# A two-layer transformer on one core: layer 1's float gate and up products from split operands, and its input norms by pairs of row tiles

## The chip, the core and the metric

The kernel runs on one core of a Trainium2 chip. TensorE (PE in the profile) multiplies matrices out of SBUF into PSUM, VectorE (DVE) and ScalarE (ACT) work element by element on both, GpSimd (POOL) does so on SBUF, and SyncE (SP) issues transfers; GpSimd's own queue issues a few as well. Each engine runs its instructions in order, and semaphores tie the engines together. The metric is the device time of one execution in microseconds, as a median of several.

## What is computed

Four sequences of 256 tokens with 256 features pass through two layers, each with a mixer and a feed-forward part, and a LayerNorm after each of the four residual sums:

```
x = layernorm(x + L0_attn(x))      16 heads, rope, softmax
x = layernorm(x + L0_ffn(x))       W2 · fwht(silu(x W1ᵀ) * (x W3ᵀ)), 1024 wide
x = layernorm(x + L1_attn(x))      an mLSTM block with an MLP of its own, below
x = layernorm(x + L1_ffn(x))       int8 weights, 1024 wide

def L1_attn(x):
    h_in  = rmsnorm(x, norm1_w)
    q, k, v, o_pre = h_in @ wq, h_in @ wk, h_in @ wv, h_in @ w_og
    i_pre, f_pre   = soft_cap(h_in @ w_ig + b_ig), soft_cap(h_in @ w_fg + b_fg)
    h     = mlstm_parallel(q, k, v, i_pre, f_pre)          # 8 heads
    h_out = sigmoid(o_pre) * (rmsnorm of each head of h * mh_w)
    x1    = x + h_out @ w_out
    h2    = rmsnorm(x1, norm2_w)
    return x1 + (silu(h2 @ w_gate) * (h2 @ w_up)) @ w_down # 256 -> 1024 -> 256
```

The change is in the last line's two products, w_gate and w_up, and in the norms that lead to h_in and h2.

## The kernel before

Tokens go in two halves, n = 0 and n = 1, of 512 tokens, that is four row tiles of 128 (NJH = 4). Residual rows are token-major (`acc[n]`, `xb[n]`, `xs[n]`), the input of a product is feature-major (`fm`, two chunks of 128 features by 512 tokens). `transposed` (L794) makes the one from the other: four transposes for each chunk on TensorE, and one eviction that multiplies by the norm's weight on VectorE (L806).

*The feed-forward parts.* `glu` (L820) goes over the eight blocks c of 128 hidden features: one float32 product of two matmuls 128x512 for the gate and one for the up part (both recorded at the helper's L70), a tanh on ScalarE (L829), two operations on VectorE (L831, L832) that leave the gated block in `hT`. `fast_glu` (L847) does the same work by a Strassen scheme: for each pair of blocks, seven products at 128x256 (L871) on sums of weights (`hidden_sums`, L165) and of tokens (`token_sums`, L835 to L841) in place of eight. Layer 0 uses `fast_glu` for its half 0 and `glu` for half 1 (`ffn0`, L941). Layer 1's MLP uses `glu` for half 0 and `fast_glu` for half 1 (`ffn1`, L963). `down` (L925) is the product back to 256 features, eight float32 matmuls 128x256 for each row tile (L930). The int8 feed-forward part at the end (`ffn2_*`, from L1286) already uses float32r products on inputs in two parts (L1279).

*Norms.* `layernorm` (L770) and `rmsnorm` (L782) work on four row tiles at a time: bn_stats or a square with a sum on ScalarE (L787) for each tile, one chain of small VectorE steps for the reciprocal roots of all four (`rsqrt`, L51: 13 steps, of which 9 are three Newton rounds), then one scaling for each tile (L777, L790). The mLSTM's input is LayerNorm, root, RMSNorm, root; h2 is an RMSNorm of the rows that the product with w_out leaves (L1269).

*The order of the work.* The streams are generators that yield an amount of TensorE time. `merge` (L1382) emits pieces of one stream between those of another: the rest of `ffn0(1)` lies under `mlstm(0)`, the downs of `ffn0(1)` around `ffn1(0)`'s norm, the blocks of `ffn1(0)` under `mlstm(1)`, its downs around the head norm of half 1 and around h2_1's norm, and `ffn1(1)` then runs by itself, followed by the int8 part. A scheduler fixes the order on each engine when the kernel is built; emission order is its priority, and `behind` and `issue_after` are explicit orders. Inside `mlstm` stand: `mlstm_in` (L1009; transposes of hin, then w_if, w_qk, w_vo), gates and decays (GpSimd's L1153 is part of these, released by the "far" transfers on SP's queue), `attend` (L1178, L1195), `head_norm` (L1208 to L1228), transposes of `hos` and the product with w_out. `mix`, `late` and `work` are SBUF pools.

*Storage.* Large weights and sums share one pool tag "ff" with seven tiles of 1 MB that go round: wsum0, xsum, wsum1, w2b, w2, w1, w3, then gsum, gsum3 with tsum, w_up, w_gate, w_down and the three int8 weights q_gate, q_up (issued on GpSimd's queue when `ffn0(1)`'s downs are emitted) and q_down. PSUM has four banks under the tags "mm" and "sc" (tag "d" of the streams) and four under "pt" and "ot" (tag "m").

Of the kernel before, what the change touches and what calls it, by code (L numbers as in the profile page):

```python
# [17 lines left out]
P = 128  # L18
# [17 lines left out]
SWAP = [i ^ 1 for i in range(32)]  # L36


@with_exitstack
def tile_two_layers(ctx: ExitStack, tc: tile.TileContext, a: dict, out: bass.AP):  # L40
# [10 lines left out]
    def rsqrt(v, n, scale, eps):  # L51

        ve = small.tile([P, n], F32, tag="rs_v", name="rs_v")
        nc.vector.tensor_scalar(ve, v, scale, eps, ALU.mult, ALU.add)
        sh = small.tile([P, n], I32, tag="rs_sh", name="rs_sh")
# [83 lines left out]
    def ff_weight(name, engine=nc.sync, dtype=F32):  # L139

        tiled = [P, NH, D] if name in ("w2", "w_down", "q_down") else [P, KC, FF]
        t = wts.tile(tiled, dtype, tag="ff", name=name, bufs=7)
# [4 lines left out]
    pair_sums = lambda k: wts.tile([P, 4, 4 * P], F32, tag="ff", name=f"wsum{k}", bufs=7)  # L147
    wsums = [pair_sums(0)]
    xsum = wts.tile([P, 2, 4, S], F32, tag="ff", name="xsum", bufs=7)
    wsums.append(pair_sums(1))  # L150
    w2b = wts.tile([P, NH, D], F32, tag="ff", name="w2b", bufs=7)
    w2, w1, w3 = (ff_weight(k) for k in ("w2", "w1", "w3"))


# [492 lines left out]
    for h in range(NB - 1):  # L647
# [3 lines left out]
        if h == NB - 3:  # L651
            gsum = wts.tile([P, 2, 2, NH // 2, P], F32, tag="ff", name="gsum", bufs=7)
            with behind(settled["block"]):
                hidden_sums(nc.vector, (w1, w3), "first")
# [11 lines left out]
    both = wts.tile([P, 8 * S], F32, tag="ff", name="gsum3", bufs=7)  # L666
# [50 lines left out]
    mix = tc.alloc_tile_pool(name="mix", bufs=1, side="right")  # L717
# [44 lines left out]
    def hidden(n, pool):  # L762
        return pool.tile([P, NH, HALF], F32, tag="hT", name=f"hT{n}")
# [18 lines left out]
    def rmsnorm(src, dst):  # L782

        ss = small.tile([P, NJH], F32, tag="rms_ss", name="rms_ss")
        for j in range(NJH):
            junk = work.tile([P, D], F32, tag="junk", name="junk")
            nc.scalar.activation(junk, src[:, j, :], AF.Square, accum_out=ss[:, j : j + 1])  # L787
        rstd = rsqrt(ss, NJH, 1.0 / D, RMS_EPS)
        for j in range(NJH):
            nc.vector.tensor_scalar(  # L790
                dst[:, j, :], src[:, j, :], rstd[:, j : j + 1], None, ALU.mult
# [28 lines left out]
    def glu(xT, wg, wu, hT, tag):  # L820

        for c in range(NH):
# [9 lines left out]
            nc.vector.tensor_tensor(hT[:, c, :], pu, g, ALU.mult)  # L832
# [14 lines left out]
    def fast_glu(xT, wg, wu, hT, tag, spare, fourth, other):  # L847
# [4 lines left out]
        def pair(k):  # L852
# [23 lines left out]
            def places(c, b):  # L876
                if not g:
                    g.append(spare(k))
                return g[0][:, c, batch(b)], hT[:, 2 * k + c, batch(b)]
# [45 lines left out]
    def down(hT, wd, j, tag, rows, scale=0.5):  # L925

        po = bank(tag)[:, :D]
        for i in range(NH):
            fill(
                lambda: nc.tensor.matmul(  # L930
                    po, lhsT=hT[:, i, j * P : (j + 1) * P], rhs=wd[:, i, :],
# [9 lines left out]
    def ffn0(n, tag):  # L941
        fm = feature_major(n)
        if not n:
            rest = hidden(2, hid)
            four = rest[:, 0:2, :].rearrange("p x (k d) -> p x k d", d=P)
            hidden_sums(nc.gpsimd, (w1, w3), "fourth", four)
        hT = hidden(n, hid)
# [5 lines left out]
        if n:  # L953
            yield from glu(fm, w1, w3, hT, tag)
        else:
            token_sums(fm)
            room = lambda k: rest[:, 2 + 2 * (k % 2) : 4 + 2 * (k % 2), :]
            yield from fast_glu(fm, w1, w3, hT, tag, room, lambda x, k: four[:, x, k], rows[0])
        for j in range(NJH):
            yield from rows[j]  # L960
        layernorm(acc[n], xb[n])

    def ffn1(n, tag):  # L963

        h2 = work.tile([P, NJH, D], F32, tag="hin", name=f"h2_{n}")
        rmsnorm(acc[n], h2)
        yield 0.0
        fm, hT = feature_major(n), hidden(n, hid)
        evicted = transposed(h2, fm, tag, vecs[:, 4:6])
        if n:  # L970
            with tc.issue_after(evicted.ins):
                evicted = token_sums(fm)
            with tc.issue_after(evicted.ins):
                evicted = hidden_sums(nc.vector, (w_gate, w_up), "fourth")
        with tc.issue_after(evicted.ins):
            for j in range(NJH):
                nc.vector.tensor_tensor(xs[n][:, j, :], acc[n][:, j, :], xb[n][:, j, :], ALU.add)
        yield 0.9
        rows = [down(hT, w_down, j, tag, xs[n][:, j, :], 1.0 if n else 0.5) for j in range(NJH)]
        if n:  # L980
            room = lambda k: split.tile([P, 4, HALF], F32, tag="qx", name="gates")[:, 0:2]
            yield from fast_glu(
                fm, w_gate, w_up, hT, tag, room,
                lambda x, k: (w_gate, w_up)[x][:, 0, (2 * k + 1) * P : (2 * k + 2) * P], rows[0],
            )
        else:
            yield from glu(fm, w_gate, w_up, hT, tag)
        for j in range(NJH):
            yield from rows[j]
# [8 lines left out]
    ones = mix.tile([2 * 32, S], F32, tag="ones", name="ones")  # L998
    nc.gpsimd.memset(ones, 1.0)
    bias = mix.tile([P, 1], F32, tag="bias", name="bias")  # L1000
    nc.scalar.mul(bias, b_if, 1.0 / CAP)
    DV = DV1 + 1
    HV = H1 * DV
    own = mix.tile([P, H1], F32, tag="own", name="own")
    nc.vector.tensor_reduce(own, ident.rearrange("p (h d) -> p h d", h=H1), AX.X, ALU.add)
# [537 lines left out]
```

## Time and profile before

| | us |
|---|---|
| three runs | 694.25, 696.74, 696.4 |
| median of them | 696.4 |
| span of the profiled execution | 692.4 |
| time around that span (696.4 less 692.4) | 4.0 |
| layer 1 begins: transposes of hin, half 0 | 460.99 |
| `ffn1(0)`: first gate product | 523.85 |
| transposes of hin, half 1 | 536.44 |
| w_qk of half 1 | 540.32 |
| last product of `attend`, half 1 | 578.1 |
| transposes of h2_1 | 597.45 |
| `ffn1(1)`: first gate product | 599.40 |
| `ffn1(1)`: last gate or up product | 626.09 |
| int8 part: first product | 638.16 |
| end of the span | 692.4 |

Times are from the start of the span. In a line of the timeline the fields are: start, length, engine, line of the kernel, operation, output and inputs, shapes, number of instructions, and in brackets the idle time before them with what ended it. A float32 matmul leaves two records, a float32r matmul one; a record's length includes its way through the array, so the time of one is read from the distance of starts. In a line of windows the fields are: window and its length, then busy time with the number of instructions of PE, PEld, DVE, ACT and POOL, then the granted TensorE clock, the DMA share and GB/s.

### The profile page before, as it was taken

The numbers are of one execution on the slowest core, as the hardware profiler recorded it, in microseconds if no ns is written. First come the engines' busy times: TensorE is split into PE (matmuls) and PEld (weight loads), VectorE is DVE, ScalarE is ACT, GpSimd is POOL, SyncE is SP. The second block draws the span as 40 slices with busy tenths as digits, with TensorE's granted clock in tenths as the row PEclk, the third lists the DMA queues.
The fourth block names the chain that finished last, engine by engine and source line by source line (L and its number), as shares of the span: only waits on it lengthen the run. The fifth ranks groups of instructions, "written<-read, shape, count | busy, mean of one in ns | idle before, by whom it ended". The sixth has DMA issues, their size and how long they took to land.

```text
span 692.4 us, 10218 instructions
## 1 busy us (share of the span) xinstructions
PE 680.3 (98%) x3504; PEld 551.4 (80%) x3504; DVE 474.0 (68%) x1310; ACT 280.2 (40%) x839; POOL 183.0 (26%) x191
## 2 busy tenths in 40 slices
PE   9999999999999999999999999999999999999995
PEld 5888988988888898898888878845685568788785
DVE  5966766666477478467747786474779648966767
ACT  2442543344254254334425355136412561261652
POOL 3254314413431440441442920004100140000210
PEclk9999999999999999999999999999999999999998
DMA  8543233232331421520331322003031300001001
GB/s 270 216 123 61 39 100 62 54 95 51 67 96 36 108 66 26 138 57 17 64 62 28 96 47 87 1 0 124 1 121 62 120 4 1 0 1 62 0 1 62
DMA packets 49030, 45.46 MB, mean 66 GB/s; under 512 B 9521, under 2 KB 42705, under 8 KB 47825
## 3 DMA queue, kind: packets, MB, share of 16 engines
q1 hardware_dynamic: 48112, 41.00, 22.8%
q0 software_dynamic: 432, 3.15, 1.3%
q10 hardware_dynamic: 432, 0.66, 0.3%
q8 instruction: 28, 0.46, 0.3%
q14 instruction: 26, 0.20, 0.1%
HBM read 25.61 MB, written 1.08 MB: 39 GB/s over the span
## 4 chain that ended last, share of the span: by engine, by line
PE 88%; DVE 8%; ACT 2%; POOL 1%; issue 1%; DVEq 0%; ACTq 0%
PE ps_mm L371 13%; PE ps_mm L70 10%; PE ps_ot L70 8%; PE ps_d L70 7%; PE ps_sc L363 6%; PE ps_sc L371 6%; PE ps_d L930 4%; PE ps_d L1279 4%; PE ps_m L70 4%; PE ps_sc L455 4%; PE ps_pt L455 4%; PE ps_m L871 4%; PE ps_d L871 3%; PE ps_sc L467 2%; PE ps_m L930 2%; PE ps_m L1195 2%
## 5 line engine op out<-in xcount | busy, mean ns | idle before, releaser
L315 POOL TENSOR_TENSOR rope_raw<-rope_raw,cst 128x512 f32<-128x512 f32 x30 | 38.2, 1272 | 181.8 <-DVE rope_swp L312 181.8
L487 ACT ACTIVATE pr<-ps_sc,nmax 128x256 f32<-128x256 f32 x64 | 29.7, 475 | 121.3 <-DVE nmax L478 121.3
L70 PE MATMUL ps_mm<-w_o,oT 128*128 128x256 f32 x256 | 62.2, 379 | 0.0
L70 PE MATMUL ps_ot<-prT,v 128*128 128x256 f32 x240 | 61.4, 380 | 0.1
L569 DVE TENSOR_TENSOR acc<-ps_mm,acc 128x512 f32<-128x512 f32 x32 | 22.1, 690 | 48.3 <-PE ps_mm L70 48.3
L70 PEld LDWEIGHTS ps_mm<-w_o,oT 128*128 128x128 f32 x256 | 46.6, 190 | 5.3
L70 PEld LDWEIGHTS ps_ot<-prT,v 128*128 128x128 f32 x240 | 43.3, 190 | 5.5 <-issue 0.8
L1153 POOL TENSOR_TENSOR ex<-cst,ex 128x512 f32<-128x512 f32 x16 | 19.7, 1266 | 93.7 <-DMA ex<-far 93.7
L385 ACT COPY kn<-ps_sc 128x256 f32<-128x256 f32 x56 | 20.9, 373 | 58.3 <-PE ps_sc L363 58.2
L497 DVE TENSOR_SCALAR pr<-pr,rinv 128x256 f32<-128x256 f32 x128 | 42.8, 375 | 1.6
L371 PE MATMUL ps_mm<-xsum,wsum 128*128 128x256 f32 x180 | 43.9, 380 | 0.0
L505 DVE STREAM_TRANSPOSE cross<-pr 128x512 f32<-128x512 f32 x60 | 42.6, 711 | 1.4
L478 DVE TENSOR_REDUCE nmax<-ps_sc 128x2 f32<-128x512 f32 x32 | 20.6, 686 | 32.7 <-PE ps_sc L467 32.6
L316 POOL TENSOR_TENSOR rope_swp<-rope_swp,cst 128x512 f32<-128x512 f32 x30 | 38.1, 1270 | 0.0
L371 PEld LDWEIGHTS ps_mm<-xsum,wsum 128*128 128x128 f32 x180 | 33.9, 190 | 4.5
L394 DVE TENSOR_TENSOR kn<-ps_sc,kn 128x256 f32<-128x256 f32 x42 | 17.8, 423 | 28.5 <-ACT kn L385 18.1
L487 ACT ACTIVATE pr<-ps_pt,nmax 128x256 f32<-128x256 f32 x64 | 30.1, 489 | 2.6 <-DVE nmax L478 2.6
L455 PE MATMUL ps_sc<-kn,qn 128*128 128x256 f32 x128 | 30.2, 379 | 0.0
L455 PE MATMUL ps_pt<-kn,qn 128*128 128x256 f32 x128 | 30.2, 379 | 0.0
L70 PE MATMUL ps_d<-fm,w 128*128 128x512 f32 x64 | 29.4, 599 | 0.0
L930 PE MATMUL ps_d<-w,hT 128*128 128x256 f32 x128 | 28.4, 379 | 0.0
L363 PEld LDWEIGHTS ps_sc<-wsum,xsum 128*128 128x128 f32 x168 | 25.4, 191 | 2.2
(317 smaller groups left out, 1631.0 us busy)
## 6 DMA issues: line engine op xcount, KB each, us to landing
prT<-cross SPq DMA_DIRECT2D x240, 64.0 KB, 2.1
w_qkv<-in_w_qkv SPq DMA_DIRECT2D x7, 1024.0 KB, 7.0
ex<-far SPq DMA_DIRECT2D x8, 512.0 KB, 5.1
w<-in_w SPq DMA_DIRECT2D x3, 1024.0 KB, 11.6
w_o<-in_w_o SPq DMA_DIRECT2D x8, 256.0 KB, 3.3
acc<-in_x SPq DMA_DIRECT2D x2, 512.0 KB, 9.0
w_up<-in_w_up SPq DMA_DIRECT2D x1, 1024.0 KB, 4.9
w_gate<-in_w_gate SPq DMA_DIRECT2D x1, 1024.0 KB
```

The lines of the kernel that those rows point to most:

```text
L70: last = nc.tensor.matmul(ps, lhsT=lhs(i), rhs=rhs(i), start=(i == 0), stop=(i == n - 1))
L315: nc.gpsimd.tensor_tensor(by_b(raw[c]), by_b(raw[c]), cs, ALU.mult)
L316: nc.gpsimd.tensor_tensor(by_b(swp), by_b(swp), sn, ALU.mult)
L363: lambda: nc.tensor.matmul(ps[:, k * S + j * P : k * S + (j + 1) * P], lhsT=x[:, j * P : (j + 1) * P], rhs=wt, start=(start and not k and ...
L371: lambda: nc.tensor.matmul(ps[:, k * S : (k + 1) * S], lhsT=wt, rhs=x, start=(start and not k), stop=True, skip_group_check=True,)
L455: lambda: nc.tensor.matmul(ps[bb][e][:, qt * S : (qt + 1) * S], lhsT=qn[:, e, queries(bb, qt)], rhs=kn[:, e, keys(bb)], start=(qt == 0), s ...
L487: nc.scalar.activation(pr[:, qt, :], ps[:, qt * S : (qt + 1) * S], AF.Exp, bias=nmax[:, qt : qt + 1], accum_out=rsum[:, qt : qt + 1],)
L497: nc.vector.tensor_scalar(pr[:, qt, :], pr[:, qt, :], rinv[:, qt : qt + 1], None, ALU.mult)
L505: return nc.vector.transpose(cross[:, :, e], pr.rearrange("p t (x i) -> p x t i", i=32))
L871: nc.tensor.matmul(banks[name][:, batch(x)], lhsT=left, rhs=right, start=start and not x, stop=True, skip_group_check=True,)
L930: lambda: nc.tensor.matmul(po, lhsT=hT[:, i, j * P : (j + 1) * P], rhs=wd[:, i, :], start=(i == 0), stop=(i == NH - 1),)
L1279: nc.tensor.matmul(ps, lhsT=lhs, rhs=rhs, start=(k == 0), stop=(k == len(terms) - 1))
```

## The change

*Split operands.* `parts_of` clears the twelve low bits of a float32 operand for its top (a bitwise AND with −4096 on VectorE) and takes the rest exactly. With T, L the top and rest of a weight and t, l those of an input, three float32r operands are kept of each: T, L and T/4096 − L; t, 4096·l and t − 4096·l. `three_products` adds T·t + L·(4096 l) in one bank (P0, four matmuls 128x512 over the two feature chunks) and the product of the third parts in another (P1, two matmuls). Then (1 + 1/4096)·P0 − P1 = T·t + T·l + L·t + L·l. ScalarE takes the first term (`mul`), VectorE subtracts the second.

*Use.* `split_glu` takes this for the gate and up products of both halves of layer 1's MLP: per block c twelve matmuls into four banks. In half 0 the gate goes on by tanh, with the last product of gate and up on GpSimd; in half 1 by a silu on ScalarE, with that product on VectorE. `fast_glu` and its sums are no longer used in layer 1.

*Weights.* w_gate and w_up come in raw by quarters into the buffers of hin (SP's queue). The gate's quarters are split when `ffn0(1)`'s first two steps have been emitted, the up part's inside the first downs of `ffn0(1)`; the subtraction of a weight's top is on GpSimd. The pool "ff" has seven fixed places: gate parts in 3, 0, 1, up parts in 2, 5, 6 (those of wsum1, w1, w3), w_down in 4, the int8 weights in 0, 1, 2. These are therefore issued when the products of `ffn1(1)` are done, all three on GpSimd's queue. `hT` is eight tiles from a pool of ten instead of one; the int8 part's `hT` lies in quarters in freed places.

*Norms.* `mlstm_rows` does the LayerNorm and the RMSNorm of the mLSTM's input for a pair of row tiles with one chain for both roots, right behind those tiles' downs. `mlp_rows` does h2's RMSNorm for a pair right behind its products with w_out. `mlstm_in`'s yield ahead of the transposes goes from 9.0 and 10.5 to 5.0, that ahead of `ffn1(1)`'s transposes from 6.0 to 4.3.

```diff
+TOP = -4096
+STEP = 2.0**-12
...
+    def slot(k, shape, name, dtype=F32):
+        return wts.tile(shape, dtype, tag=f"ff{k}", name=name)
...
-    w_up, w_gate = ff_weight("w_up"), ff_weight("w_gate")
+    def raw_weights(name):
+        staged = [work.tile([P, 2, KC, S], F32, tag="hin", name=f"raw_{name}") for _ in range(2)]
+        quarters = [t[:, k] for t in staged for k in range(2)]
+        for q, t in enumerate(quarters):
+            nc.sync.dma_start(t, a[name][:, :, q * S : (q + 1) * S])
+        return quarters
+    raw_gate = raw_weights("w_gate")
...
+    def parts_of(src, to, scaled, engine):
+        low, fine = to[1], to[2]
+        top = work.tile([P, HALF], F32, tag="glu_t", name="top")
+        top = top.rearrange("p (a b) -> p a b", b=src.shape[-1]) if len(src.shape) == 3 else top
+        nc.vector.tensor_single_scalar(top.bitcast(I32), src.bitcast(I32), TOP, ALU.bitwise_and)
+        if scaled:
+            nc.vector.tensor_tensor(src, src, top, ALU.subtract)
+            nc.scalar.mul(low, src, 1.0 / STEP)
+            nc.vector.tensor_tensor(fine, top, low.bitcast(F32), ALU.subtract)
+        else:
+            engine.tensor_tensor(low, src, top, ALU.subtract)
+            nc.vector.scalar_tensor_tensor(fine, top, STEP, low.bitcast(F32), ALU.mult, ALU.subtract)
+        nc.scalar.copy(to[0], top)
+    def weight_parts(raw, to, q):
+        parts_of(raw[q], [t[:, :, q * S : (q + 1) * S] for t in to], False, nc.gpsimd)
+    def input_parts(fm):
+        x = work.tile([P, 3, KC, HALF], F32R, tag="parts", name="parts", bufs=1)
+        for c in range(KC):
+            parts_of(fm[:, c, :], [x[:, k, c, :] for k in range(3)], True, nc.vector)
+        return x
+    def three_products(ps, w, x, c):
+        cols = slice(c * P, (c + 1) * P)
+        for at, ks in ((0, (0, 1)), (1, (2,))):
+            terms = [(w[k][:, i, cols], x[:, k, i, :]) for i in range(KC) for k in ks]
+            for m, (left, right) in enumerate(terms):
+                last = nc.tensor.matmul(ps[at], lhsT=left, rhs=right, start=(m == 0), stop=(m == len(terms) - 1))
+        return last
+    def whole(dst, ps):
+        nc.scalar.mul(dst, ps[0], 1.0 + STEP)
+        nc.vector.tensor_tensor(dst, dst, ps[1], ALU.subtract)
+    def split_glu(x, wg, wu, hT, tag, smooth):
+        for c in range(NH):
+            pg, pu = [bank(tag) for _ in range(2)], [bank(tag) for _ in range(2)]
+            fill(lambda: three_products(pg, wg, x, c))
+            yield 1.35
+            fill(lambda: three_products(pu, wu, x, c))
+            z = work.tile([P, HALF], F32, tag="glu_g", name="glu_g")
+            nc.scalar.mul(z, pg[0], 1.0 + STEP)
+            with behind(weighed[-1]) if weighed and not smooth else contextlib.nullcontext():
+                nc.vector.tensor_tensor(z, z, pg[1], ALU.subtract)
+            if smooth:
+                nc.scalar.activation(z, z, AF.Silu)
+                whole(hT[c], pu)
+                nc.vector.tensor_tensor(hT[c], hT[c], z, ALU.mult)
+            else:
+                g = work.tile([P, HALF], F32, tag="glu_t", name="glu_t")
+                evictions.append(nc.scalar.activation(g, z, AF.Tanh, scale=0.5))
+                whole(hT[c], pu)
+                nc.vector.scalar_tensor_tensor(z, g, 1.0, z, ALU.add, ALU.mult)
+                nc.gpsimd.tensor_tensor(hT[c], hT[c], z, ALU.mult)
+            yield 1.35
...
+    def mlstm_rows(n, j):
+        if n not in entry:
+            entry[n] = work.tile([P, NJH, D], F32, tag="hin", name=f"hin{n}")
+        mv = small.tile([P, 2, 2], F32, tag="ln_mv", name="in_mv")
+        for k in range(2):
+            statistics(acc[n][:, j + k, :], mv[:, k, :])
+        ve = small.tile([P, 4], F32, tag="rs_v", name="rs_v")
+        nc.vector.tensor_scalar(ve[:, 0:2], mv[:, :, 1], 1.0 + RMS_EPS, RMS_EPS * LN_EPS, ALU.mult, ALU.add)
+        nc.vector.tensor_scalar(ve[:, 2:4], mv[:, :, 1], LN_EPS, None, ALU.add)
+        y = root(ve, 4)
...
+    def mlp_rows(n, j):
...
+            nc.scalar.activation(junk, acc[n][:, j + k, :], AF.Square, accum_out=ss[:, k : k + 1])
+        rstd = rsqrt(ss, 2, 1.0 / D, RMS_EPS)
...
     def ffn0(n, tag):
...
-            yield from glu(fm, w1, w3, hT, tag)
+            for k, wait in enumerate(glu(fm, w1, w3, hT, tag)):
+                if k == NH:
+                    raw_up = raw_weights("w_up")
+                yield wait
+            kept["up"] = [slot(k, [P, KC, FF], f"up{k}", F32R) for k in (2, 5, 6)]
...
         for j in range(NJH):
-            yield from rows[j]
-        layernorm(acc[n], xb[n])
+            for wait in rows[j]:
+                if n and j < 2:
+                    weight_parts(raw_up, kept["up"], splits.pop(0))
+                yield wait
+            if j % 2:
+                mlstm_rows(n, j - 1)
...
     def ffn1(n, tag):
-        rmsnorm(acc[n], h2)
-        yield 0.0
-        evicted = transposed(h2, fm, tag, vecs[:, 4:6])
...
+        transposed(mlp[n], fm, tag, vecs[:, 4:6])
+        x = input_parts(fm)
...
+        yield from split_glu(x, kept["gate"], kept["up"], hT, tag, bool(n))
...
+            if j % 2:
+                mlp_rows(n, j - 1)
...
-    merge(chain(take(1, one), [4.3]), other)
+    merge([4.3], other)
...
-    w_down = ff_weight("w_down")
-    q_gate, q_up = (ff_weight(k, nc.gpsimd, F32R) for k in ("q_gate", "q_up"))
+    w_down = ff_weight("w_down", 4)
...
-    merge(chain(take(1, one), [6.0]), left)
+    merge([4.3], left)
+    run(take(1, one))
     run(left)
-    run(take(1 + len(STEPS), one))
-    q_down = ff_weight("q_down", nc.gpsimd, F32R)
+    run(take(2 * NH, one))
+    q_gate, q_up, q_down = (ff_weight(name, k, nc.gpsimd, F32R) for k, name in enumerate(("q_gate", "q_up", "q_down")))
```

More of the change, by code (lines that the diff above doesn't have):

```diff
@@ L651, in tile_two_layers @@
         if h == NB - 3:
[L652 removed]
+            gsum = slot(0, [P, 2, 2, NH // 2, P], "gsum")
             with behind(settled["block"]):
@@ L959, in ffn0 @@
+            yield from fast_glu(fm, w1, w3, hT, tag, gates, lambda x, k: four[:, x, k], rows[0])
         for j in range(NJH):
-            yield from rows[j]
-        layernorm(acc[n], xb[n])
-    def ffn1(n, tag):
-        h2 = work.tile([P, NJH, D], F32, tag="hin", name=f"h2_{n}")
-        rmsnorm(acc[n], h2)
-        yield 0.0
-        fm, hT = feature_major(n), hidden(n, hid)
-        evicted = transposed(h2, fm, tag, vecs[:, 4:6])
[L970 to L977, printed above, removed]
-        yield 0.9
[L979 to L987, printed above, removed]
@@ L988, in ffn1 @@
         for j in range(NJH):
-            yield from rows[j]
+            yield from down(hT, w_down, j, tag, xs[n][:, j, :], 1.0 if n else 0.5)
             if j % 2:
                 layernorm(xs[n][:, j - 1 : j + 1], xb[n][:, j - 1 : j + 1], 2)
[L998 to L1004, printed above, removed]
@@ L1096, in gates @@
         nc.vector.tensor_scalar_mul(neg, last, -1.0)
-        summed = nc.vector.tensor_tensor(lsp, fcum, gmax, ALU.add)
-        if n:
-            with behind(summed):
-                hidden_sums(nc.vector, (w_gate, w_up), "first")
+        nc.vector.tensor_tensor(lsp, fcum, gmax, ALU.add)
         nc.scalar.activation(fac[:, 0:P], g[:, 0:P], AF.Exp, bias=neg)
```

112 lines of the change are left out of this document (68 added, 44 removed).

## The prediction

> **What bounds the kernel now.** I read the busy table first, then the chain that ended last, then that chain in order of time over layer 1, then TensorE's timeline at the stages that the diff touches, and the clock in the tail.
>
> ```profile
> PE 680.3 (98%) x3504; PEld 551.4 (80%) x3504; DVE 474.0 (68%) x1310; ACT 280.2 (40%) x839; POOL 183.0 (26%) x191
> ...
> PE 88%; DVE 8%; ACT 2%; POOL 1%; issue 1%; DVEq 0%; ACTq 0%
> ```
>
> TensorE is the bound over the whole span, so a product saved is time saved wherever its stage has no other chain of the same length. The second look is at those places:
>
> ```profile
> 597.45 1.13 PE ps_m L799 x7
> 598.60 0.76 DVE fm L806
> 599.40 8.32 PE ps_m L871 x36
> 607.83 14.81 PE ps_m L871 x68
> 622.64 1.73 PE ps_m L930 x8
> 624.37 1.73 PE ps_m L871 x8
> ...
> 645.80 16.37 PE ps_d L1279 x72
> ```
>
> The columns are start, length, engine, tile, line, records. The reader is to see that the second half's gate and up products (L871) are one run of TensorE, entered through one eviction of VectorE (L806), and that the int8 FFN's products, already float32r, come at 16.37/72 = 0.2274 us.
>
> ```profile
> 523.85 1.99 PE L70 MATMUL ps_d<-fm,w_gate 128*128 128x512 f32 x4 [0.41 <-DVE fm L806]
> 525.67 1.88 PE L70 MATMUL ps_d<-fm,w_up 128*128 128x512 f32 x4
> 527.39 1.88 PE L70 MATMUL ps_d<-fm,w_gate 128*128 128x512 f32 x4
> ...
> 597.45 1.23 PE L799 MATMUL ps_m<-cst,h 128*128 128x128 f32 x8 [0.90 <-DVE h L790]
> 598.51 0.60 PE L1292 MATMUL ps_d<-cst,xb 128*128 128x128 f32 x4
> 599.40 0.70 PE L871 MATMUL ps_m<-fm,w_gate 128*128 128x256 f32 x2 [0.30 <-DVE fm L806]
> ```
>
> In the first half a float32 block (gate or up, one of 16) takes 527.39 − 525.67 = 1.72 us. Idle time of TensorE is small and lies exactly where the change puts more work on VectorE: 0.41 and 0.30 us before the two GLUs, 0.90 before h2_1's transposes.
>
> **The change, part by part** (line numbers are those of the kernel before; prices not shown above are means of its groups by shape).
>
> 1. *Products, first half.* Sixteen blocks of 1.72 = 27.5 us become sixteen of six float32r matmuls, 96 x 0.2274 = 21.8: **−5.7**.
>
> 2. *Products, second half.* Before, 8.32 + 14.81 + 1.73 and 0.11 between them = 24.97 us (seven products instead of eight, at 128x256). After, again 21.8: **−3.1**. Had the seven-product form gone on in the first half too, there would be less to save; as it is the two sum to −8.8.
>
> 3. *Weight parts.* A quarter of a weight is a bitwise AND on VectorE, a subtraction on GpSimd, one fused op on VectorE, one copy on ScalarE. Prices: L790 (128x256, SBUF to SBUF, scalar operand) comes every 0.285 us, so 0.57 for 512; the fused op as L831, 0.68; the subtraction as L1153 on GpSimd, 1.27; the copy as the cast L1295, 0.59. The four gate quarters (VectorE 5.0, GpSimd 5.1 us) are issued beside layer 0's second GLU, where VectorE is busy 8.6 of the 10.3 us from 449.7 and 27.1 of the 45 after it: the second stretch covers them, 0; without it 5.0. The up quarters take the tiles of w1 and w3, whose last product is at about 504, so in the built order their steps stand in VectorE's queue between the root and the gating of mLSTM half 0's head norm, and hos's second pair of transposes waits behind one quarter's AND and fused op: 0.57 + 0.68 = 1.25, **+1.2** (bounds 0, if the downs in TensorE's queue cover it, and 5.0 for four quarters).
>
> 4. *Input parts, first half.* Behind each eviction come AND 0.57, a subtraction 0.68, a scaling on ScalarE 0.59, a subtraction 0.68 and a copy 0.59. The first product needs eviction, AND and copy: 1.16 more than now; the corrections follow 1.9 us behind it. Eight downs (8 x 0.43 = 3.45 us) stand before it in the built order. I take 0.4 for the start and 0.6 for the wait on the corrections: **+1.0** (0.4 to 2.4).
>
> 5. *Norms by pairs.* The mLSTM's LayerNorm and RMSNorm share one root, and nothing is left between the last down and the transposes but one pair. The 0.30 us before hin1's transposes goes, since 4.5 pairs of blocks now fit ahead of them: **−0.4** with the neighbouring 0.1 (0 to −0.9).
>
> 6. *Cover in mLSTM half 1.* Before, eight blocks, 13.8 us, fill its waits; after, by my walk, 41 matmuls, 9.3 us. That is where the first half's saving is cashed, if the stage's own chain allows it. VectorE is busy 22.7 of its 37.8 us and ScalarE 21.1, so neither is the limit by throughput; but single 0.23-us matmuls now stand where a 1.72 block covered a VectorE step, and hT's product of gate and up is on GpSimd behind eight L1153 of 1.27. I take **+0.6** (0 to +4.5, all of the lost cover).
>
> 7. *Entry of the second half's GLU.* In the built order VectorE runs two rows of xb0, one residual add and one bn_stats between the two pairs' roots; h2_1 ends some 0.8 later than now, 599.0. Then evictions 2 x 0.70, AND 0.57, copy 0.59: first product at about 602.2 instead of 599.4, last correction of the second chunk at 604.8, and four products of 0.2274 behind it: the first pair of blocks ends at 605.7. Seven pairs of 2.73 end at 624.8; undelayed from 599.4 they would end at 621.2. That is 3.6; two of the steps overlap by records' tails of 0.1 to 0.2, so **+3.3** (1.2, the bare eviction-AND-copy, to 4.5).
>
> 8. *Evictions.* A pair of blocks takes TensorE 2.73, ScalarE three ops of 0.6 (1.8), VectorE three of 0.69 (2.07), GpSimd 1.27: TensorE remains longest, 0. Were VectorE held up by over 0.66 us in each pair it would be the bound.
>
> 9. *Removed:* sums for seven products (L172 and its kin, eight of 0.68 on VectorE), token sums (L838 to L841), copies: all beside TensorE's run, 0. *Moved transfers:* w_up and w_gate raw in quarters on SP's queue ahead of the far transfers; the three q weights on GpSimd's queue behind the GLU instead of far ahead. A q weight lands 4.8 us after its issue (4.6 for q_down), and the second half's downs give 32 x 0.43 = 13.8 us cover; q_gate and q_up need 4.8 to 9.6: 0 (one behind the other and late: +1).
>
> Sum: −5.7 − 3.1 + 1.2 + 1.0 − 0.4 + 0.6 + 3.3 = **−3.1**. The profiled execution spans 692.4 us and has about 4.0 around it, 696.4, which is the median shown (694.25 to 696.74). So 696.4 − 3.1 = **693.3 us**.
>
> A rule against the change comes from what GpSimd newly does: eight subtractions and eight products, 16 x 1.27 = 20 us, beside VectorE's steps. The trace has such a meeting:
>
> ```profile
> 408.61 2.13 DVE L838 TENSOR_TENSOR gsum<-fm 128x256 f32<-128x256 f32 x1
> 410.66 0.41 DVE L840 TENSOR_TENSOR gsum<-fm 128x256 f32<-128x256 f32 x1
> ```
>
> ```profile
> 407.97 2.49 POOL L177 TENSOR_TENSOR hT<-w,gsum 128x512 f32<-128x512 f32 x2
> ```
>
> The same VectorE operation took 2.13 us while two GpSimd operations ran, and 0.41 after them: 1.72 lost, once. My sum has 0 for this; its bound is 1.27 a meeting. [...]
>
> [...]
>
> **The rivals.**
>
> *The whole saving comes through.* The splits hide under downs, mLSTM half 1's waits are as short as its engines' busy shares (60% and 56%) suggest, and the entry costs only its bare steps: −5.7 − 3.1 − 0.4 + 0.4 + 0 + 1.2 = −7.6, **688.8 us**. For it: the head norms have downs in TensorE's queue. Against: VectorE and GpSimd are in order, and the built order has the up parts before the gating.
>
> *mLSTM half 1 is a chain.* The 4.5 us of cover that go were filling waits that stay; the stage ends at 578 as before. Then +4.5 in place of +0.6: −3.1 + 3.9 = +0.8, **697.2 us**. For it: TensorE shows nearly no idle time there only because the blocks fill it. Against: the walk finds filler left at every larger wait.
>
> *Slower: the lock between VectorE and GpSimd on the path.* Place: the four up subtractions inside head norm 0 and the four or five products of the first half's GLU beside hin1's root and h_0's split. Eight or nine meetings of 1.27 would add 10.2 to 11.4; −3.1 + 10.2 = +7.1, **703.5 us** at the full price. It is slower than before from three meetings on the path (3.8), and by more than 0.5% from six. Against: a root's steps last 0.2 us, and most meetings fall where TensorE has work.
>
> *Slower, smaller: the clock.* Between h2_1's transposes (end about 599.7) and 602.2 TensorE would stand 2.5 us. The tail shows what idling does:
>
> ```profile
> 685.00:687.00 2.00, 0.00 (x0) 0.00 (x0) 1.97 (x8) 0.60 (x1) 0.00 (x0) 1.00 0.15 50
> 687.00:689.00 2.00, 0.00 (x0) 0.00 (x0) 1.53 (x9) 0.63 (x2) 0.00 (x0) 0.65 0.25 81
> ```
>
> Last matmul at 684.8, granted clock 1.00 to 687, 0.65 in the next window, 0.50 after it (the column before the last two): it fell about 2.8 us after the last product. A gap of 2.8 would start the GLU at half clock; how long that lasts no row shows, between 0 and its 21.8 us (+21.8 at most). At five pairs of blocks it would be 5 x 2.73 = +13.7: **707 us**; at one, +2.7: **696 us**.
>
> **How the numbers follow.** A measurement of this kernel tells some 0.5% from no change, 3.5 us here: faster is under 692.9, slower over 699.9. Forecast 0.45 (its own range 689.5 to 697, split 0.22 faster, 0.23 same); whole saving 0.24 (faster); chain in mLSTM 0.08 (0.06 same, 0.02 slower); lock 0.17 (0.16 slower, 0.01 same); clock 0.06 (slower but for 0.01). That is 0.46 faster, 0.31 same, 0.23 slower. The range goes down to the products' whole saving with no stall anywhere, 696.4 − 8.8 − 0.9 = 686.7, and up to six meetings of the lock on top of the forecast, 693.3 + 7.6 = 700.9.
>
> **What would show it.** Products: six float32r matmuls of 0.227 a block, 2.73 us a pair, in both halves. Step 3: idle time of TensorE at hos's second pair, released by VectorE behind an AND or fused op of the up parts. Steps 4 and 7: start of the two GLUs relative to their transposes, 1.2 us more, then a wait on ScalarE's or VectorE's parts. Step 6: time from w_qk to the last attend, 37.8 now, 33.7 after. The lock: two-input VectorE operations of 1 us and more beside GpSimd's. The clock: under 1.00 after the gap. The prediction is wrong if any of these is off by over 3 us, the lock and step 6 above all.

## The result and the profile after

The changed kernel takes 702.76 us (median of four runs, 702.12 to 703.59) against 695.33 for the kernel before on the same chip: a ratio of 1.0111, 95% interval 1.0090 to 1.0132. It is slower by 7.7 us by that ratio (7.4 by the medians); forecast were 693.3 us and a range up to 701. Its profiled execution spans 700.4 us (692.4 before).

From the page of the changed kernel, busy times and the chain's shares:

```profile
PE 677.8 (97%) x3520; PEld 556.3 (79%) x3520; DVE 487.6 (70%) x1348; ACT 294.9 (42%) x839; POOL 204.8 (29%) x207
...
PE 81%; DVE 11%; ACT 2%; issue 1%; DMA 1%; POOL 1%; SPq 1%; POOLq 0%; ACTq 0%; DVEq 0%
```

TensorE's busy time fell by 2.5 us (680.3 before), where the two product steps together said 8.8; its idle time rose from 12.1 to 22.6 us. The chain has lost 7 points of TensorE and gained 3 of VectorE. Where the idle time lies is read from TensorE's timeline of the changed kernel (idle before the group and what ended it in brackets):

```profile
512.14 0.66 PE L902 MATMUL ps_m<-cst,xs 128*128 128x128 f32 x4 [1.76 <-DVE xs L1305]
...
515.79 3.86 PE L76 MATMUL ps_m<-w_out,fm 128*128 128x256 f32 x16 [1.70 <-DVE fm L909]
...
542.84 0.44 PE L902 MATMUL ps_m<-cst,hin 128*128 128x128 f32 x2 [1.11 <-DVE hin L878]
...
592.66 0.66 PE L902 MATMUL ps_m<-cst,xs 128*128 128x128 f32 x4 [1.50 <-DVE xs L1305]
...
607.78 0.79 PE L816 MATMUL ps_m<-parts,gate 128*128 128x512 f32 x1 [2.52 <-ACT parts L797]
```

The first four are waits for a norm or its eviction on VectorE: the second pair of hos and the eviction of hos in half 0, hin of half 1, hos of half 1. The fifth is the entry of the second GLU, where two evictions and an AND on VectorE and a copy on ScalarE stand one behind the other. Three smaller waits, 0.65 us in half 0's products (for ScalarE's low part) and 0.81 and 0.66 before h2_1's transposes, bring the sum to 10.7 us. By stages, from the same timelines (us; "rounded" is the last version below):

| stage | before | changed | forecast change | change | rounded |
|---|---|---|---|---|---|
| start to `ffn1(0)`'s first product | 523.9 | 528.8 | +1.6 | +4.9 | 524.6 |
| from there to the last product of `attend`, half 1 | 54.3 | 52.9 | −4.9 | −1.4 | 49.0 |
| from there to `ffn1(1)`'s first product | 21.2 | 26.1 | +2.8 | +4.9 | 22.3 |
| from there to the int8 part | 38.8 | 38.8 | −2.6 | 0.0 | 36.8 |
| rest | 54.2 | 53.8 | 0 | −0.4 | 53.7 |

The changed kernel's stages begin at these lines:

```profile
528.80 0.59 PE L816 MATMUL ps_d<-parts,gate 128*128 128x512 f32 x1
...
581.65 9.07 PE L1033 MATMUL ps_d<-w_down,hT 128*128 128x256 f32 x40
...
646.57 1.28 PE L1358 MATMUL ps_d<-qx,q_gate 128*128 128x512 f32 x4
```

Each of the first four stages missed its forecast by 2 to 3.5 us on the same side, 11 us in all.

The first stage's loss in VectorE's and GpSimd's timelines of the changed kernel:

```profile
503.90 0.17 DVE L62 TENSOR_SCALAR rs_sh<-rs_v 128x16 int32<-128x16 int32 x1
504.11 1.28 DVE L64 TENSOR_SCALAR rs_y<-rs_sh 128x16 int32<-128x16 int32 x1
505.31 0.16 DVE L65 TENSOR_SCALAR rs_v<-rs_v 128x16 f32<-128x16 f32 x1
505.43 1.20 DVE L68 TENSOR_TENSOR rs_t<-rs_y 128x16 f32<-128x16 f32 x1
```

```profile
504.09 2.50 POOL L795 TENSOR_TENSOR up<-raw_w_up,top 128x512 fp32r<-128x512 f32 x2 [5.04 <-DVE rs_sh L62]
510.62 3.81 POOL L795 TENSOR_TENSOR up<-raw_w_up,top 128x512 fp32r<-128x512 f32 x2 [4.03 <-DVE top L789]
```

Two steps of head norm 0's root, 0.17 us elsewhere, last 1.28 and 1.20 while GpSimd subtracts. Later it is GpSimd that is slow (3.81 for two), and the chain in order of time shows who waits for it:

```profile
510.62 2.60 POOL up L795
513.25 1.73 DVE up L796
514.98 1.32 DVE fm L909 x2
```

The eviction of hos (L909) stands in VectorE's queue behind the third part of an up quarter, and that waits for GpSimd. At the other end, by windows (the third column from the right is the granted clock):

```profile
604.00:608.00 4.00, 0.92 (x5) 0.62 (x6) 3.81 (x16) 0.89 (x2) 0.00 (x0) 0.67 0.00 0
608.00:612.00 4.00, 4.00 (x9) 2.77 (x10) 2.87 (x9) 2.06 (x4) 0.00 (x0) 0.50 0.02 4
612.00:616.00 4.00, 4.00 (x19) 3.23 (x18) 2.44 (x4) 3.60 (x5) 0.00 (x0) 0.97 0.00 0
```

```profile
605.00:606.00 1.00, 0.26 (x3) 0.03 (x1) 0.84 (x4) 0.00 (x0) 0.00 (x0) 0.70 0.00 0
```

The second GLU begins at half clock: its first pair of blocks takes from 607.78 to 612.82, 5.0 us, the later ones 2.81. Windows of 1 us show 1.00 up to 605, 0.50 from 606 to 612 and 0.89 in the next, so the clock was low from about 605.4 to 612.2, 6.8 us.

### The profile page after: what moved, and what is told of

Read it like the earlier page. It is cut to its first block, busy times and chain, and to the rows that moved or that the text cites. A ratio compares the mean times of both kernels' runs of the same rounds, so it can differ in the third digit from the quotient of the medians.

```text
span 700.4 us, 10351 instructions
## 1 busy us (share of the span) xinstructions
PE 677.8 (97%) x3520; PEld 556.3 (79%) x3520; DVE 487.6 (70%) x1348; ACT 294.9 (42%) x839; POOL 204.8 (29%) x207
## 4 chain that ended last, share of the span: by engine, by line
PE 81%; DVE 11%; ACT 2%; issue 1%; DMA 1%; POOL 1%; SPq 1%; POOLq 0%; ACTq 0%; DVEq 0%
PE ps_mm L378 13%; PE ps_mm L76 9%; PE ps_ot L76 8%; PE ps_sc L370 6%; PE ps_sc L378 6%; PE ps_pt L462 4%; PE ps_sc L462 4%; PE ps_d L1358 4%; PE ps_m L816 4%; PE ps_d L816 3%; PE ps_sc L474 2%; PE ps_d L76 2%; PE ps_m L1033 2%; PE ps_m L1272 2%; PE ps_d L974 2%; PE ps_pt L474 2%
## 5 line engine op out<-in xcount | busy, mean ns | idle before, releaser
L504 DVE TENSOR_SCALAR pr<-pr,rinv 128x256 f32<-128x256 f32 x128 | 39.3, 348 | 1.6
```

The lines of the kernel that those rows point to most:

```text
L504: nc.vector.tensor_scalar(pr[:, qt, :], pr[:, qt, :], rinv[:, qt : qt + 1], None, ALU.mult)
```

## The experiments

Microseconds against the changed kernel are differences of the ratios to the kernel before times 694.5. A ratio's interval is ±0.9 to ±2.1 us; a difference to the changed kernel has two of them in it, about ±2 us (1.8 to 2.5), so differences of 1.5 to 2.5 us are hardly clear of noise. The effects overlap and don't add up.

One more thing moves the times: the granted clock falls in other places too, and not in the same ones in every version. Ahead of the end of the span, where it falls too (from 687 in the kernel before), it was low for 6.8 us in the trace of the changed kernel (at 605), for none in those of the kernel before, `half0_float`, `warm`, `rounded` and `rounded_early`, but for 10.2 in `product_vector`, 13.6 in `up_sub_vector`, 17.1 in `norms_whole` and 20.4 in `no_gpsimd` (sums of windows of 1 us, with 0.50 taken as the lower value). For instance, in `product_vector` and then in `norms_only`, with TensorE busy all the time:

```profile
564.00:569.00 5.00, 5.00 (x22) 4.28 (x23) 2.38 (x5) 1.69 (x5) 2.56 (x3) 0.66 0.00 0
```

```profile
562.00:566.00 4.00, 4.00 (x17) 1.92 (x14) 3.27 (x8) 0.83 (x2) 0.00 (x0) 0.57 0.00 0
```

The shortest of these stretches last 3.4 us. In that time at a clock of 0.50 TensorE loses up to 1.7 us (an estimate, half of 3.4), as much as several of the differences below.

**The norms by themselves, and the products by themselves.** `norms_only` puts `mlstm_rows` and `mlp_rows` into the kernel before; `norms_whole` takes them out of the changed one:

```diff
-            if j % 2:
-                mlstm_rows(n, j - 1)
+        layernorm(acc[n], xb[n])
...
-            if j % 2:
-                mlp_rows(n, j - 1)
...
+        rmsnorm(xb[n], hin)
+        yield 10.5 if n else 9.0
```

> The kernel before with the norms by pairs alone, products as before (float32 and seven-product form). If the pairs pay: 0.5 to 1.5 us under the kernel before's 695.3. If the two interleaved roots are the longer chain: 0.5 to 2.5 us over it. If the stalls before hin1's and h2_1's transposes are set elsewhere: within 0.5.

> The changed kernel with the split products but the norms of four row tiles at a time, as before, with their old places in the order. Theory 'the pairs' interleaved roots lengthen the chains to hin1 and h2_1': faster than the changed kernel by 1 to 3 us, 700 to 702. Rival 'the pairs pay, and without them the loss would be larger': 704 to 708.

`norms_only`: 0.9973 (0.9959 to 0.9986), 1.9 us under the kernel before. `norms_whole`: 1.0260 (1.0234 to 1.0287), 18 us over it. The pairs pay in both kernels; the loss lies with the products and their splits, and it would be larger without the pairs. That the pairs are worth 10 us beside the split and 2 without it was expected by neither theory; with whole norms TensorE's idle time is 26.7 us, spread over ten waits of 0.3 to 3.6 us in layer 1, and the clock is low for 17.1 us instead of 6.8. Which of these weighs most was not separated.

**The split of the up parts.** `up_is_gate` neither loads nor splits w_up, `up_loaded` loads it:

```diff
-            kept["up"] = [slot(k, [P, KC, FF], f"up{k}", F32R) for k in (2, 5, 6)]
+            kept["up"] = kept["gate"]
...
-                if n and j < 2:
-                    weight_parts(raw_up, kept["up"], splits.pop(0))
```

> The changed kernel without any split of w_up: the up products read the gate's parts (w_up is neither loaded nor split, so the output is not the reference's). Theory: the split of the up parts inside mLSTM half 0's head norm costs the two idle stretches of TensorE there, 1.76 and 1.70 us, and some of the 1.1 us before: 698.5 to 699.5. Rival: the head norm's delay comes from the three GLU blocks of ffn0(1) that now stand there and from the norms by pairs; then 701.5 to 703.

> As up_is_gate, but w_up is still loaded, and the three int8 weights wait for the end of the second half's GLU as in the changed kernel, so that no transfer moves forward into layer 0 (in up_is_gate 2.8 us of TensorE's time went there, at 380 to 390). What is left out is only the split of w_up; the up products read the gate's parts. Theory: the split's place in the head norm costs what its two idle stretches show, 3.46 us, less what comes back later: 699 to 701 (2 to 3.5 under the changed kernel). Rival 'given back to later chains': 702 to 703.

`up_is_gate` came out like the changed kernel, 1.0112 (1.0086 to 1.0139): the head norm's idle time was gone, but an int8 weight's place was free early, and TensorE now idled 2.8 us at 380 to 390 in layer 0. So it said nothing until that was kept out. `up_loaded`: 1.0043 (1.0025 to 1.0061), 4.7 us less. That is no less than the 3.46 us of idle time; in the trace, hos's first transposes to the GLU's first product take 15.6 us instead of 19.5.

**GpSimd or VectorE.** Where a step on VectorE lasts longer beside GpSimd's work than elsewhere (L64 1.28 us against 0.17), the text calls it the lock. `no_gpsimd` moves the up subtractions and the GLU's products to VectorE, `up_sub_vector` and `product_vector` only one of them:

```diff
-                nc.gpsimd.tensor_tensor(hT[c], hT[c], z, ALU.mult)
+                nc.vector.tensor_tensor(hT[c], hT[c], z, ALU.mult)
...
-                    weight_parts(raw_up, kept["up"], splits.pop(0))
+                    weight_parts(raw_up, kept["up"], splits.pop(0), nc.vector)
```

> The changed kernel with the eight products of the first half's GLU and the four subtractions of the up parts on VectorE instead of GpSimd. Theory 'lock': the VectorE steps of 0.8 to 1.3 us beside GpSimd (L64 1.28, L68 1.20, L796 1.73, later L64 0.81, L68 0.81, L878 1.30, L69 1.24) go back to 0.16 to 0.68, some 5 us of chain in all, against 12 x 0.6 us of new VectorE work of which 2 to 3 us lie on the path: 698 to 701, so 2 to 5 us under the changed kernel's 702.8. Rival 'queue': what delays is the work in VectorE's queue ahead of the chains, whoever else runs; more of it makes the kernel slower, 703 to 706.

> The changed kernel with only the four subtractions of the up parts on VectorE instead of GpSimd. Theory 'lock': in the head norm VectorE's L64 (1.28 us), L68 (1.20) and L796 (1.73) fall to 0.17 and 0.68, the wait for GpSimd ahead of the eviction goes, and 4 x 0.6 us of VectorE work come: the idle 3.46 us before w_out of half 0 fall under 1, and the kernel is 1 to 2.5 us faster than changed, 700 to 701.8. Rival 'queue': four more operations in VectorE's queue cost more than the lock: 703 to 704.5.

> The changed kernel with only the eight products of half 0's GLU on VectorE instead of GpSimd, 8 x 0.6 us. Theory 'queue': this is what made no_gpsimd slower (its second head norm began 1.4 us later than in the changed kernel though its first product of half 0 was 1.3 earlier): 704 to 706.5. Rival 'lock': the blocked steps beside these products (L64 0.81, L68 0.81, L878 1.30, L69 1.24) weigh more: 700.5 to 702.

1.0147 (1.0122 to 1.0171), 1.0076 (1.0049 to 1.0103) and 1.0141 (1.0117 to 1.0165): +2.5, −2.4 and +2.1 us against the changed kernel. The traces say more than these times. In the head norm of half 0 the root's steps are back at 0.17 us in `up_sub_vector`. From the start of the downs under it to the product with w_out pass 10.2 us in the changed kernel, 8.7 in `up_sub_vector` and in `no_gpsimd`, and 6.1 in `up_loaded`; to the GLU's first product 23.2, 22.0 and 19.1. So the move gains 1.2 of the 4.2 us that the split costs up to this product, and that is the lock's cost on the path less what the four subtractions cost on VectorE; the two were not separated. The two idle stretches are gone (ten more matmul records of downs stand between the pairs of hos), but 1.33 us stand ahead of that product in their place:

```profile
516.79 3.62 PE L76 MATMUL ps_m<-w_out,fm 128*128 128x256 f32 x16
...
530.08 0.50 PE L816 MATMUL ps_d<-parts,gate 128*128 128x512 f32 x1 [1.33 <-ACT parts L797]
```

The execution traced is the slowest of the four (702.52 us at a mean clock of 0.987); the fastest took 697.81 at 0.993, the clock of the changed kernel.

In the GLU the cure gains nothing: hin's second pair is ready 14.5 us after the GLU's first product in `product_vector` and 14.3 in the changed kernel, so there three more operations of VectorE weigh as much as the steps that GpSimd held up. That they weigh more, as the theory 'queue' has it, is not shown. The traced execution spans 1.8 us more than the changed kernel's, and it loses them between the GLU's first product and the last one of `attend` (54.7 against 52.9), where the window at 564 above has the low clock: sixteen matmuls of `attend` and six of the GLU take 4.94 us there, 3.19 at full clock in the changed kernel (from 575.36).

```profile
563.26 2.42 PE L1272 MATMUL ps_m<-va,ex 128*128 128x33 f32 x16 [0.74 <-DVE ex L1263]
565.49 2.91 PE L816 MATMUL ps_d<-parts,gate 128*128 128x512 f32 x6
568.20 1.63 PE L816 MATMUL ps_d<-parts,up 128*128 128x512 f32 x6
```

The clock is likewise a rival for the 2.5 us of `no_gpsimd`. Whether the 0.74 us of idle time brought the low clock on was not tried.

**One half in float32.** `half0_float` and `half1_float` multiply one half in float32 by the weights' tops:

```diff
-        x = input_parts(fm)
+        x = input_parts(fm) if n else None
...
+            yield from glu(fm, kept["gate"][0].bitcast(F32), kept["up"][0].bitcast(F32), hT, tag)
```

> The changed kernel with half 0's gate and up products in float32 on the top parts (their low parts are left out there), and half 1 as changed. TensorE needs 16 x (1.72 - 1.41) = 5.0 us more. Theory 'VectorE's queue': as much comes back (idle before hin1's and hos's transposes 1.76 and 1.50, scattered waits of 2 in mLSTM half 1): 701 to 704. Rival 'the split pays in half 0 by its products': 706 to 708.

> The changed kernel with half 1's gate and up products in float32 on the top parts (their low parts left out), evicted as in half 0 of the kernel before. TensorE needs 27.5 us where the changed kernel's stage took 25.1 from the first to the last product; the entry loses its AND, copy and corrections, 2.6 us, and the half clock: theory 'entry': 701 to 704, no gain from the split in half 1. Rival: the split pays there: 705 to 707.

`half0_float`: 1.0008 (0.9993 to 1.0023), 7.1 us faster than the changed kernel with 5.0 us more for TensorE. `half1_float`: 1.0132 (1.0102 to 1.0162), 1.5 slower, within the noise. In half 0 the split loses far more than its products give; part of that is the clock, which stays at 1.00 at the second GLU of `half0_float` (600 to 612). Its timeline also shows where the second half's gap went:

```profile
593.13 5.34 PE L1033 MATMUL ps_d<-w_down,hT 128*128 128x256 f32 x24
598.31 1.04 PE L902 MATMUL ps_m<-cst,h 128*128 128x128 f32 x8
599.18 3.62 PE L1033 MATMUL ps_d<-w_down,hT 128*128 128x256 f32 x16
602.45 0.58 PE L816 MATMUL ps_m<-parts,gate 128*128 128x512 f32 x1
```

With longer GLU blocks left over, these cover the head norm, and 40 records of downs remain to cover h2_1's norm and split. In the changed kernel the blocks are used up when `attend` ends, 48 of 64 records go before w_out, and 16 are left for the longest wait.

**TensorE's time in half 0.** `half0_longer` does one matmul of each block three times:

```diff
+            for left, right in terms[: again * at]:
+                nc.tensor.matmul(ps[at], lhsT=left, rhs=right, start=True, stop=True)
```

> The changed kernel with two more float32r matmuls in each block of half 0 (the third-part product's first matmul is done three times, the first two overwritten), 32 in all, 32 x 0.234 = 7.5 us of TensorE, everything else alike. Theory 'VectorE's and ScalarE's chains set half 0's pace': most of it falls into idle time, 702 to 705. Rival 'TensorE sets it': 709 to 711.

1.0190 (1.0169 to 1.0211): 5.5 of the 7.5 us come through, between the two theories and nearer to TensorE. Half 0 is not a stage bound by VectorE throughout, in which TensorE's time would be free; it is TensorE's stage with single stalls.

**The clock.** `warm` fills the gap, one idle matmul after the transposes of two row tiles and five after the last:

```diff
+            warm(crossed[-7], 1)
+            warm(crossed[-1], 5)
```

> The changed kernel with six idle float32 matmuls of 128x256 (0.43 us each, into an unused bank) between h2_1's transposes and the second half's first product, so that TensorE isn't idle for over 2 us there. Theory 'clock': the granted clock stays at 1.00 and the first pair of blocks takes about 3.5 instead of 5.0 us: 700.5 to 701.8. Rival 'the corrections set the pace': within 0.7 of 702.8.

1.0085 (1.0061 to 1.0109), 1.8 us less, with an interval that just takes in nothing. The trace is clearer: the first product comes 0.6 later (608.35), and the first pair of blocks takes 3.5 us instead of 5.0. Its windows keep the clock:

```profile
604.00:608.00 4.00, 3.98 (x22) 2.95 (x20) 3.81 (x21) 0.32 (x1) 0.00 (x0) 1.00 0.02 6
608.00:612.00 4.00, 3.30 (x13) 2.35 (x14) 3.75 (x12) 3.23 (x7) 0.00 (x0) 1.00 0.00 0
```

**Cheaper parts.** `one_bank` adds T·t + L·t + T·l in one bank, with the same 192 matmuls; `rounded` and `rounded_early` also make the parts by a cast:

```diff
+        terms = [(w[k][:, i, cols], x[:, m, i, :]) for k, m in ((0, 0), (1, 0), (0, 1)) for i in range(KC)]
...
+        nc.scalar.copy(high, raw[q])
+        engine.tensor_tensor(low, raw[q], high.bitcast(F32), ALU.subtract)
...
+            nc.scalar.mul(x[:, 0, c, :], pt, weight[:, c : c + 1])
+            nc.vector.scalar_tensor_tensor(
+                x[:, 1, c, :], pt, weight[:, c : c + 1], x[:, 0, c, :].bitcast(F32), ALU.mult, ALU.subtract
+            )
```

> The changed kernel with another three-pass sum: T·t + L·t + T·l added up in one bank of PSUM (the product of the two low parts, some 2^-24 of the whole, is left out), so the same 192 float32r matmuls, but no third parts, no scaling and subtraction at the eviction, and the gated product is evicted as in the plain float32 GLU: per pair of blocks VectorE 1.37 instead of 2.07 us, ScalarE 0.6 instead of 1.8, GpSimd nothing. Theory 'VectorE's queue': the products' gain was lost to evictions and splits ahead of the norms' chains; the idle time after layer 0 falls from 11 to under 5 us and the kernel ends at 690 to 695. Rival 'TensorE': float32r products mixed with float32 ones and the clock eat the gain; then 699 to 703.

> As one_bank (T·t + L·t + T·l in one bank), with parts made by rounding: ScalarE casts the operand to float32r, VectorE subtracts the cast from it; for the inputs both read the transposes in PSUM, so that the first product waits for one ScalarE operation of 0.6 us. The up parts lie in places that are free after ffn0(0)'s GLU and are made right behind hin of half 0, not in the head norm; no GpSimd. q_gate and q_up are loaded when ffn0(1) is done, as before. Theory 'VectorE's queue and the place of the up split': from one_bank's 698.9 the 2.45 us before ffn0(1)'s transposes, the 2.7 at hos and some 1.5 at half 1's entry go: 690 to 694. Rival 'the product's gain only uncovers other chains': 695 to 698.

> rounded_early with the up parts back in the head norm of mLSTM half 0, in the places of wsum1 and w1, and the int8 weights as in the changed kernel; the subtractions stay on VectorE. If the place of the up split matters with the cheaper split too, it comes out 1.5 to 3.5 us over rounded_early's 688.5: 690 to 692. If the cheap split is all that counts: 688 to 689.5.

`one_bank`: 1.0052 (1.0032 to 1.0071), 4.1 us less than changed, though not the 8 to 13 expected: the waits in half 0's products and before hin and hos of half 1 are gone (0.1 of 3.3 us), but a new 2.45 us stands ahead of `ffn0(1)`'s transposes, where the gate parts meet GpSimd (two ANDs of 1.47 and 1.49 us beside its subtractions). `rounded_early`: 0.9909 (0.9886 to 0.9932), 688.54 us; `rounded`: 0.9912 (0.9897 to 0.9928), 688.56 us. Both beat both kernels, the kernel before by 6 us, of which the norms by pairs alone are worth 1.9 (`norms_only`). The new sum, the cast, the parts read from PSUM and GpSimd's absence came in together, so the 10 us below `one_bank` are theirs jointly. The up split in the head norm, which costs 4.7 us with three parts and GpSimd, costs nothing there with a cast and one subtraction. In `rounded` the second GLU's first product waits 0.67 us instead of 2.52:

```profile
595.91 0.50 PE L811 MATMUL ps_m<-parts,gate 128*128 128x512 f32 x1 [0.67 <-ACT parts L800]
```

## Why the prediction was wrong

The bound was read rightly, and so was the list of places; the sizes of the steps were not, and the rivals held too little.

- *Products (steps 1 and 2), −8.8.* This is the largest wrong term. By the distances of starts, waits that the profile shows left out, the float32 forms held TensorE for 53.0 us; the 192 float32r matmuls held it for 49.0 in the changed kernel, not 43.7, so the gain was 4.0. (In `rounded` the same number holds it for 46.6.) One part is the spacing: 16.87/72 = 0.2343 us in this GLU, where I took 0.2274 from the int8 part (+1.3). One is the first pair of half 1 (+2.2, of which `warm` puts 1.5 down to the half clock). The rest I put down to single products between float32 ones (two took 0.43 and 0.44 us to the next start, at 545.39 and 559.09) and to small waits for corrections.
- *Up parts (step 3), +1.2.* `up_loaded` gives 4.7. I counted one quarter's AND and fused op ahead of the gating; the eviction behind a fused op that itself waits for GpSimd was in the same built order, and I put it at nothing; the 4.7 lies inside the bounds I gave (0 to 5.0). By the traces of `up_sub_vector` and `no_gpsimd`, 1.2 of 4.2 us go when GpSimd's subtractions go to VectorE, so most of it is the split's place in VectorE's queue.
- *Input parts, norms, cover (steps 4 to 6), +1.2 together.* The stage from the first GLU to the last `attend` gained 1.4 us instead of 4.9. Step 5's −0.4 was wrong in sign: TensorE waits 1.11 us before hin's transposes of half 1. Eight VectorE operations of the new evictions, 0.6 us each, stand between the root's steps, and three of the norm's own steps are held up beside GpSimd's products (L64 and L68 0.81 us, L878 1.30), so that hin's second pair is ready 14.3 us after the GLU's first product. In `one_bank`, with fewer operations for parts and evictions and without those products, it is ready after 8.4, and TensorE has no wait there. Step 8 compared a pair of blocks with its own evictions alone and left out the norms that run beside them: VectorE is busy 14.8 of the 15 us from 530 to 545.
- *Entry of the second GLU (step 7), +3.3.* Right in kind. From the last `attend` to the first product it is +4.9: a blocked root step in head norm 1 (L69, 1.24 us beside GpSimd's last product) and a GLU eviction that waits 1.51 us for its tanh ahead of that head norm come on top, then the entry's 2.5.
- *Rivals.* The lock showed in the trace (L64 1.28 us beside GpSimd, 0.17 in `up_sub_vector`) and was held at a chance of 0.17. That its 703.5 us came so near the 702.8 measured is luck: it is the sum of eight or nine meetings of 1.27 us each, the length of GpSimd's operation and not a measured loss (the six steps of norms named here lost 0.57 to 1.11: L64 1.11 and 0.64, L68 1.03 and 0.65, L878 0.57, L69 1.07), while moving the work off GpSimd gave back 1.2 us ahead of the first GLU, by the traces, and nothing for hin of half 1. The clock, held at 0.06, did fall ahead of the second GLU and was worth 1.8 us by `warm`, but not by the timing that I read from the end of the span, 2.8 us after the last product: it fell at about 605.4, 0.1 us after the last transposes and 3.0 after the downs and transposes before 602.4 that kept TensorE full. The rival that mLSTM half 1 is a chain had the right idea in the wrong stage: it is the chain after it that the saved blocks no longer cover. Its figure for that stage, −1.0 us, is near the −1.4 measured by luck, as TensorE was idle for 0.1 us in all from 545 to 580. I gave each rival a case of its own; they came together.

What the prediction would see the lock by, two-input operations of 1 us and more, showed in the row of L68, which took 1.20 us beside GpSimd. But L64 above has one input and took 1.28, and in `one_bank` an AND, with one input too, took 1.47 beside GpSimd's subtractions:

```profile
436.20 1.47 DVE L788 TENSOR_SCALAR top<-raw_w_gate 128x512 int32<-128x512 int32 x1 [0.48 <-POOL gate L790]
```

The price of the AND in step 3 I took from a row of another operation (L790), and was wrong to: the AND's own rows in the changed kernel, in the groups by shape, are

```profile
L789 DVE TENSOR_SCALAR top<-fm 128x512 int32<-128x512 int32 x4 | 1.7, 420 | 0.0
```

0.42 us each, with the next operation 0.34 after its start (510.12 and 510.46), where I had 0.57. By that price my sum would have been lower still, and further from the time measured.

## What to carry to other kernels

Where a product is made faster by splitting its operands, count what the split adds to the engine that runs the norms, in the order in which it is queued, and beside everything else that this engine does in that stage; here the faster product also took cover away from the chains behind it. Choose the form of the split by its evictions and parts first: with the same 192 matmuls, three forms here lie 14 us apart. And look at what stands in a queue behind an operation that waits for another engine: here L796 waited 0.83 us for GpSimd's 2.60 at 510.62 and lasted 1.73, and the eviction of hos behind it began at 514.9. Before two versions that differ by 2 us are explained by their work, see whether they ran at the same granted clock (`product_vector` 0.990 and the changed kernel 0.993 in the traced executions, with 10.2 and 6.8 us low).

## What was not expected of the hardware

- The granted clock of the changed kernel fell though TensorE was not quite idle: from 602 to 605.4 it was busy for 1.8 us. In `warm`, with 2.97 us of work from 600 to 604 and 3.98 from 604 to 608, it stayed at 1.00. In the changed kernel it came back at 612.2, 4.4 us after the products had begun.
- A gap alone did not decide: `one_bank` waits 2.59 us at the same place and keeps 1.00, and in `norms_only` the clock fell at 562, after 17 us in which TensorE was idle for 0.05. Ahead of the end of the span the low stretches last some 3.4 us (`norms_only`, `one_bank`) or close to two, three or four times that (6.8 in the changed kernel, by the stages' means some 10 from 604 in `no_gpsimd` and some 14 from 608 in `norms_whole`). What sets them off was not tried.
- A one-input integer step of 16 elements (L64) took 1.28 us beside GpSimd against 0.17 elsewhere, much like the two-input L68 (1.20 against 0.17).
- Float32r matmuls of 128x512 came every 0.2343 us in this GLU and every 0.2272 (16.36/72) in the int8 part of the same execution. What makes the difference was not tried.
